# Layer 3's weight product of a four-layer graph network by two levels of Strassen, with weight factors streamed from DRAM

## The chip, the core and the metric

The kernel runs on one of the eight cores of a Trainium2 chip, in float32 throughout. The metric is the device time of that core for one launch, in microseconds (us); lower is better. Five engines work side by side, each through its own queue in order: TensorE (PE, the matrix unit, with its weight loads shown apart as PEld), VectorE (DVE), ScalarE (ACT), GpSimd (POOL), and SyncE (SP), which here only issues DMAs.

## The reference, cut to what matters

Input x holds 128 graphs of 64 nodes with 512 features; adj holds a 64x64 matrix for each graph. Four residual layers follow one another, each as `x = x + layer(relu(layernorm(x)), adj)`. The change concerns layer 3, of which this is the reference:

```python
Xw = X @ Wv + bv
sj = Xw @ aw[:d, 0]
si = Xw @ aw[d:, 0]
e = jax.nn.leaky_relu(sj[:, None, :] + si[:, :, None] + ab[0], negative_slope=0.2)
alpha_matrix = A * jnp.exp(e)
transition = alpha_matrix / (jnp.sum(alpha_matrix, axis=-1, keepdims=True) + 1e-12)
for k in range(Wk.shape[0]):            # 3
    H = H + Xk @ Wk[k] + bk[k]
    Xk = jnp.einsum('bij,bjd->bid', transition, Xk)
return jax.nn.relu(H)
```

So layer 3 multiplies the 512 features of X, of T X and of T T X (T is the transition matrix of a graph) by three 512x512 weights and adds the three. For a token that is one product of a row of 1536 numbers with a 1536x512 matrix.

## The kernel before

Tokens are worked on in 16 groups of 8 graphs: 512 tokens, four tiles of 128 tokens (two graphs each). Phase 1 runs layers 0 and 1 for all groups and writes x to DRAM (`xmid`, shown as xm in the profile). Phase 2 loads it group by group, runs layers 2 and 3, and stores the output. Weights of phase 1 lie in two areas of SBUF, `WA` and `WB`; phase 2 loads its own over them: WA then holds layer 2's, WB layer 3's (`w3_sb`, lines 247 and 248).

All large weight products use one level of Strassen's scheme in Winograd's form (`strassen`, line 589; `seven`, line 568): seven block products instead of eight, and some additions. For layer 3 the two rows of blocks are two token tiles, the block columns are the halves of the 1536 inputs (6 chunks of 128), and the weight's column halves are 256 wide. Each of the seven products is thus 6 matmuls of a 128x128 stationary operand (the transposed activations, tile `a3`) and a 128x256 moving one (the weights), summed in one PSUM bank (line 607). `layer3` calls it twice for each group, for tiles 0 and 1 and for tiles 2 and 3. The left operands are formed on DVE before each call (`comb`, line 599, four additions of 768 elements). Results leave PSUM through ACT (line 575) and DVE (lines 577, 579, 991); POOL adds the bias (line 987); DVE applies the relu and adds x (line 992), which has stayed in SBUF since the group was loaded for layer 2; then SP stores the tile (line 995). The right operands are formed once, at the start of phase 2 (`combine`, line 384), and stay in SBUF.

The order of instructions is not that of the Python loops. Each operation is recorded as a node with an engine, a planned duration (`c_mm` for matmuls, `c_v` for VectorE), its tiles and a priority: the group's number times a period, plus a hand-set shift for each part of the work (table `AT`). `Graph.run` (line 82) then plays the queues through with these durations, gives tiles their slots, and writes every engine's instructions in the planned order, so work of neighbouring groups and layers is interleaved. SP's DMAs are in this plan as well, one queue in order: a DMA whose tile isn't free yet holds back those behind it. Where the planner sees PE without work for over half a microsecond, `fill` (line 1009) writes matmuls on a constant tile. Slots that phase 2 takes over from phase 1 are listed in `TWO`: the second list of each pair may be used when the last user of the first is done.

Two steps take work to another layout. `transposed` (line 551) turns a 128x512 tile by an ACT copy into 16-bit planes, a DMA transpose and an ACT copy back; layers 2 and 3 use it for each token tile. In layer 3 `lm` (line 973) makes T X and T T X, transposed, with 64-row matmuls.

Of the kernel before, what the change touches and what calls it, by code (L numbers as in the profile page):

```python
# [14 lines left out]
P = 128  # L15
# [3 lines left out]
T = 4  # L19
# [148 lines left out]
def tile_adj_preln_d4(  # L168
# [25 lines left out]
        ([("tmp", [P, D], 4), ("mB", [P, T, C + 1], 1)], [("s3", [P, 3, 6, P], 1)]),  # L194
        ([("z", [P, DH], 2)], [("hT", [P, KD, T * P], 1)]),
        ([("rT", [P, KH, P], 3)], [("vu", [P, 2, D + 1], 2), ("tt", [P, T, 2, C], 2)]),
        ([("s2", [P, 3, 4, P], 1), ("s1", [P, 3, 2, P], 2)], [("a3", [P, 3 * KD, P], 2)]),
        ([("y", [P, D], 2)], [("qT", [P, 2, 2 * P], 2)]),
        ([("mT", [P, KD, P], 3)], [("a3", [P, 3 * KD, P], 1)]),
        ([("row", [P, D], 4)], [("sh", [P, 4, 2, 2 * P], 1)]),  # L200
        ([("wa", [P, D], 1)], [("q", [P, D], 1)]),
    ]
# [29 lines left out]
    WB = const.tile([P, 10752], F32, name="wb_mem")  # L232
# [6 lines left out]
    w2_sb = view(WB, 0, KH, D)  # L239
    w2_x = view(WB, 4096, 3 * 4, D // 2).rearrange("p (i c) o -> p i c o", i=3)  # L240
    w_sb = view(WB, 7168, KD, D)
    w_x = view(WB, 9216, 3 * 2, D // 2).rearrange("p (i c) o -> p i c o", i=3)
# [4 lines left out]
    w3_sb = view(WB, 0, 3 * KD, D)  # L247
    w3_x = view(WB, 6144, 3 * 6, D // 2).rearrange("p (i c) o -> p i c o", i=3)


    def c_mm(n, count):
        return 2 * count * max(n * 2 / 2400 + 0.0025, 0.111)
# [21 lines left out]
    def quad(b):  # L274
# [5 lines left out]
    STRETCH, PERIOD1, PERIOD2 = (2.11, 6.43, 4.5, 0.21), 79.8, 140.53  # L280
    AT = {
        "x0": -1458.56, "apart": 58.27, "w1": -1207.06, "b1": -1268.61, "w2": 312.2, "w": -214.25, "c1": 103.95,
        "l0": -1592.46, "c2": -560.69, "l1": 125.29, "c": 849.04, "g0": -1279.86, "g1": -1456.39, "g2": -589.08,
        "g3": -1259.16, "g": -1258.76, "bq": 321.93, "l3": 56.2, "wg": 1603.23, "w3": 387.13, "beg0": -72.8,
        "beg1": 73.58, "end00": 0.51, "end01": 19.09, "end11": -75.14, "new2": 31.64, "new3": 4.77, "end2": -39.58,
        "end3": -21.31, "load1": -108.19, "load2": 27.97, "m": 12.29, "h0": 9.53, "p0": 10.98, "z0": -29.14,
        "q0": 15.48, "y0": -518.61, "h1": -26.33, "p1": -22.59, "z1": -30.25, "q1": 4.48, "y1": -2.94, "s": -20.64,
# [63 lines left out]
    def x_mid(g, t):  # L351
        return xmid[g, t], [("xmid", g, t)]
# [12 lines left out]
    load_w("w2", w2_sb, W2T)  # L365
    b2_b = load_row(b2)
    part("w")
    load_w("w", w_sb, w)


    wa_b = Buf("wa")
# [758 lines left out]
```

## Time and the profile before

| What | Value |
|---|---|
| Median of three runs | 2377.02 us (2373.26 to 2377.84) |
| Span of the profiled execution, first to last instruction | 2373.3 us |
| PE busy | 2349.7 us, 99% of the span |
| DVE busy | 1742.1 us, 73% |
| ACT busy | 1268.7 us, 53% |
| POOL busy | 958.7 us, 40% |
| DMA traffic | 171.02 MB, mean 72 GB/s |
| Chain that ended last | PE 89%; matmuls of line 607 alone 61% |

The span is what the engines show; the time of a run is the device's own. A busy share counts an engine's instructions only, not its waits. Each float32 matmul of the source appears as two MATMUL records and two LDWEIGHTS records. The duration in a record includes the passage through the array, so that records of matmuls overlap; what one costs in a stream is the distance from its start to the next start. The groups of instructions name the tiles by their program names, joined with an underscore where two phases share memory (`tmp_mB_s` holds layer 3's sums in phase 2). The steady part of phase 2 runs from about 1465 us to 2110 us, nine groups.

### The profile page before, as it was taken

The numbers are of one execution on the slowest core, as the hardware profiler recorded it, in microseconds if no ns is written. First come the engines' busy times: TensorE is split into PE (matmuls) and PEld (weight loads), VectorE is DVE, ScalarE is ACT, GpSimd is POOL, SyncE is SP. The second block draws the span as 40 slices with busy tenths as digits, with TensorE's granted clock in tenths as the row PEclk, the third lists the DMA queues.
The fourth block names the chain that finished last, engine by engine and source line by source line (L and its number), as shares of the span: only waits on it lengthen the run. The fifth ranks groups of instructions, "written<-read, shape, count | busy, mean of one in ns | idle before, by whom it ended". The sixth has DMA issues, their size and how long they took to land.

```text
span 2373.3 us, 33860 instructions
## 1 busy us (share of the span) xinstructions
PE 2349.7 (99%) x12008; PEld 1867.5 (79%) x12008; DVE 1742.1 (73%) x3798; ACT 1268.7 (53%) x1746; POOL 958.7 (40%) x1514
## 2 busy tenths in 40 slices
PE   9999999999999999999999999999999999999999
PEld 4677677777677776677788888888888888888887
DVE  7888778788778788777868566666666766667764
ACT  4566656567565576565745445444445444454422
POOL 6244455544455444555443323333323333323330
PEclk9999999999999999999999999999999999999999
DMA  7333222333223333232532322213322223322211
GB/s 258 80 80 65 54 68 64 71 80 63 50 68 69 72 80 54 55 73 71 133 106 59 76 69 61 69 45 69 76 64 65 64 52 73 71 63 65 48 36 40
DMA packets 336922, 171.02 MB, mean 72 GB/s; under 512 B 284656, under 2 KB 290672, under 8 KB 336752
## 3 DMA queue, kind: packets, MB, share of 16 engines
q1 hardware_dynamic: 336752, 168.86, 29.5%
q8 instruction: 94, 1.54, 0.3%
q14 instruction: 76, 0.62, 0.1%
HBM read 66.99 MB, written 34.70 MB: 43 GB/s over the span
## 4 chain that ended last, share of the span: by engine, by line
PE 89%; DVE 5%; DMA 3%; ACT 1%; issue 1%; POOL 1%; SPq 1%; DVEq 0%; ACTq 0%
PE ps L607 61%; PE ps L845 14%; PE ps L546 4%; PE ps L911 2%; PE ps L758 2%; PE ps L973 2%; PE ps L878 1%; DMA x<-xm 1%; DVE st L516 1%; PE ps L957 0%; DMA rw<-row 0%; PE ps L705 0%; DVE tmp_mB_s L599 0%; DVE o L381 0%; PE ps L467 0%
## 5 line engine op out<-in xcount | busy, mean ns | idle before, releaser
L537 ACT ACTIVATE h<-x,nm,rs 128x512 f32<-128x512 f32 x384 | 300.2, 810 | 399.6 <-POOL nm L524 366.8
L607 PE MATMUL ps<-wb_mem,s_s_a 128*128 128x256 f32 x2184 | 512.0, 380 | 0.3
L607 PEld LDWEIGHTS ps<-wb_mem,s_s_a 128*128 128x128 f32 x2184 | 409.5, 190 | 74.0 <-issue 19.8
L518 POOL TENSOR_SCALAR rs<-mv 128x1 f32<-128x1 f32 x320 | 99.2, 310 | 493.0 <-DVE mv L517 477.5
L607 PE MATMUL ps<-wb_mem,tmp_mB_s 128*128 128x256 f32 x1152 | 262.4, 380 | 3.2 <-DVE tmp_mB_s L599 3.1
L607 PEld LDWEIGHTS ps<-wb_mem,tmp_mB_s 128*128 128x128 f32 x1152 | 218.1, 190 | 35.3 <-DVE tmp_mB_s L599 5.4
L607 PE MATMUL ps<-wb_mem,mT_a 128*128 128x256 f32 x1016 | 242.0, 380 | 0.0
L607 PE MATMUL ps<-wa_mem,mT_a 128*128 128x512 f32 x512 | 237.3, 595 | 3.9 <-ACT mT_a L548 3.9
L607 PE MATMUL ps<-wb_mem,rT_vu_tt 128*128 128x256 f32 x1024 | 238.2, 380 | 0.6 <-ACT rT_vu_tt L557 0.6
L607 PEld LDWEIGHTS ps<-wb_mem,rT_vu_tt 128*128 128x128 f32 x1024 | 192.8, 191 | 41.3 <-issue 12.5
L607 PEld LDWEIGHTS ps<-wb_mem,mT_a 128*128 128x128 f32 x1016 | 192.2, 190 | 31.8 <-issue 5.7
L516 DVE BATCH_NORM_STATS2 st<-x 128x6 f32<-128x512 f32 x256 | 173.6, 678 | 45.8 <-DMA x<-xm 40.6
L519 POOL TENSOR_TENSOR rs<-rs,mhalf 128x1 f32<-128x1 f32 x320 | 193.3, 604 | 26.4
L607 PEld LDWEIGHTS ps<-wa_mem,mT_a 128*128 128x128 f32 x512 | 97.1, 190 | 112.7 <-issue 102.4
L607 PE MATMUL ps<-wa_mem,s_s_a 128*128 128x512 f32 x384 | 180.7, 593 | 0.3 <-DVE z_hT L627 0.3
L987 POOL TENSOR_TENSOR u<-u,bk_b 128x256 f32<-128x256 f32 x96 | 76.4, 796 | 238.9 <-DVE u L579 170.2
L575 ACT COPY u<-ps 128x256 f32<-128x256 f32 (+1 forms) x160 | 72.7, 454 | 177.8 <-PE ps L845 105.1
L635 POOL TENSOR_TENSOR u<-u,row_sh 128x256 f32<-128x256 f32 x96 | 74.9, 789 | 228.1 <-DVE u L577 211.6
L733 ACT ACTIVATE z_hT<-z_hT 128x512 f32<-128x512 f32 x128 | 79.6, 627 | 157.8 <-DVE z_hT L627 157.8
L557 ACT COPY rT_vu_tt<-z_hT 128x1024 uint16<-128x1024 uint16 x128 | 147.1, 1159 | 13.7 <-DMA z_hT<-tmp_mB_s 13.3
L546 PEld LDWEIGHTS ps<-bd,h 128*128 128x128 f32 x1024 | 131.1, 192 | 26.6 <-issue 22.2
L524 POOL TENSOR_SCALAR nm<-mv,rs 128x1 f32<-128x1 f32 x320 | 138.5, 433 | 31.1
(174 smaller groups left out, 4336.0 us busy)
## 6 DMA issues: line engine op xcount, KB each, us to landing
x<-in_x_dram SPq DMA_DIRECT2D x64, 256.0 KB, 2.7
xm<-x SPq DMA_DIRECT2D x64, 256.0 KB, 2.1
x<-xm SPq DMA_DIRECT2D x64, 256.0 KB, 2.8
out_dram<-x SPq DMA_DIRECT2D x64, 256.0 KB, 2.0
adj<-in_adj_dram SPq DMA_DIRECT2D x32, 256.0 KB, 4.0
rw<-row SPq DMA_DIRECT2D x94, 64.0 KB, 2.8
wb_mem<-in_Wk_dram SPq DMA_DIRECT2D x6, 512.0 KB, 5.3
tmp_mB_s<-in_Wk_dram SPq DMA_DIRECT2D x8, 256.0 KB, 3.1
```

Of the source, the lines that this page charges most:

```text
L516: dve(0.69, lambda i=i: nc.vector.bn_stats(st.t[:, i, :], src(i)), [r[i]], [(st, i)])
L518: pool(0.32, lambda: nc.gpsimd.tensor_scalar_add(rs.t, mv.t[:, 1:2], EPS), [mv], [rs])
L519: pool(0.65, lambda: nc.gpsimd.tensor_tensor(rs.t, rs.t, mhalf, ALU.pow), [rs], [rs])
L524: pool(0.47, lambda: nc.gpsimd.tensor_scalar(nm.t, mv.t[:, 0:1], rs.t, -1.0, op0=ALU.mult, op1=ALU.mult), [mv, rs], [nm])
L537: act(0.82, lambda: nc.scalar.activation(h.t, xx.t, AF.Relu, bias=nm.t, scale=rs.t), [xx, nm, rs], [h])
L546: nc.tensor.matmul(quad(p)[:, c, :], h.t[:, c * P:(c + 1) * P], rhs(), start=True, stop=True)
L557: act(1.16, lambda: nc.scalar.copy(u16(dst()).rearrange("p c (k q) -> p c k q", q=2), u16(back()).rearrange("p (q c r) -> p c r q", q=2, c ...
L607: nc.tensor.matmul(p.t[:, :n], lhs()[:, c, :], rhs(c), start=first and c == 0, stop=c == kc - 1, skip_group_check=True)
L635: pool(0.75, lambda: nc.gpsimd.tensor_add(U.t[:, iv], U.t[:, iu], row()[:, cols]), [u, krow], [v])
L733: act(0.63, lambda: nc.scalar.activation(z.t[:, cols], z.t[:, cols], AF.Relu), [(z, j)], [(z, j)])
L845: nc.tensor.matmul(pair(p.t)[:, o, :], a, b, start=first and o == 0 and c == 0, stop=c == 1, skip_group_check=True)
L987: pool(0.88, lambda: nc.gpsimd.tensor_add(U.t[:, iv], U.t[:, u[1]], add()), [u, ka], [v])
```

## The change

Layer 3's product becomes two nested levels of Strassen for all four token tiles of a group together, and everything it needs changes with it:

- The outer level's rows are the pairs of tiles (0, 1) and (2, 3), its columns the two 256-wide halves of the 512 features in each of X, T X, T T X. The inner level has the two tiles of a pair and the 128-wide halves of those. There are 7 outer products (`product`), each of 7 inner ones, each of those 3 matmuls of 128x128 by 128x128: 147 for a group.
- A product's seven inner results go to two PSUM banks, four and three blocks of 128 columns. The outer sums are made by further accumulation in these banks: chain X takes products 1, 6, 5 and 3, chain Y products 2, then 7 and 4. ACT copies the intermediate states of X out (`snapshot`), DVE adds the Y states to them (`plus`), POOL does the inner sums and the bias (`emit`, five additions), and DVE does relu and residual.
- Left operands: DVE forms some outer blocks (`minus`, 768 elements, six instructions) and three inner ones for each product (384 elements). Two sums that Strassen needs are made before the transposition, on `h` (half tiles; tile 1, tile 3 and the pair 2, 3).
- Right operands: 49 weight factors of 384x128. In phase 1 `setup_w3` loads the pieces of Wk, forms the factors on POOL in two new slots `wp`, and writes them to DRAM (`fac`). Each product loads two blocks, of 768 KB and 576 KB, into three slots `wf`. WB, the weight loads and the `combine` at the start of phase 2 go.
- x is loaded a second time in phase 2, before layer 2 adds its result to it, so that the slot of the first load is free after the layer norm.
- Slots: phase 1's `rT` goes from 3 to 2; the new layer 3 tiles take over memory from others; WB becomes the tags `w2m` and `wm`, whose successors `a3` and `wf` may start when all of phase 1's uses of them are over.
- The planner's constants are new: the matmul cost, periods, stretches and the table `AT`, and with them the order of everything, in phase 1 too.

```diff
     TWO = [
-        ([("tmp", [P, D], 4), ("mB", [P, T, C + 1], 1)], [("s3", [P, 3, 6, P], 1)]),
+        ([("tmp", [P, D], 4), ("mB", [P, T, C + 1], 1)], [("xi", [P, 3, 3, P], 2)]),
-        ([("rT", [P, KH, P], 3)], [("vu", [P, 2, D + 1], 2), ("tt", [P, T, 2, C], 2)]),
-        ([("s2", [P, 3, 4, P], 1), ("s1", [P, 3, 2, P], 2)], [("a3", [P, 3 * KD, P], 2)]),
+        ([("rT", [P, KH, P], 2), ("wp", [P, 4, P], 2)], [("vu", [P, 2, D + 1], 2), ("tt", [P, T, 2, C], 2)]),
+        ([("s2", [P, 3, 4, P], 1), ("s1", [P, 3, 2, P], 2)], [("zz", [P, 8, P], 3)]),
...
-        ([("mT", [P, KD, P], 3)], [("a3", [P, 3 * KD, P], 1)]),
+        ([("mT", [P, KD, P], 3)], [("sx", [P, 2, 3, 2 * P], 1)]),
...
+        ([("w2m", [P, 7168], 1), ("wm", [P, 3584], 1)], [("a3", [P, 3, KD, P], 4), ("wf", [P, 4, 3, P], 3)]),
...
-        return 2 * count * max(n * 2 / 2400 + 0.0025, 0.111)
+        return 2 * count * max(n * 2 / 2400 + 0.0045, 0.1115)
...
-    STRETCH, PERIOD1, PERIOD2 = (2.11, 6.43, 4.5, 0.21), 79.8, 140.53
+    STRETCH, PERIOD1, PERIOD2 = (2.6483, 3.2376, 6.9527, 0.0065), 98.8, 156.601
...
-        return xmid[g, t], [("xmid", g, t)]
+        return xmid[g, t], [("xmid", g, t)] + ([("xo", g - 1, t)] if g else [])
...
+        bkv = bk3_b.rearrange("p (j n c) -> p j n c", j=2, n=2)
+        dve(0.42, lambda: nc.vector.tensor_sub(bkv[:, :, 1], bkv[:, :, 1], bkv[:, :, 0]), ["bk3"], ["bk3"])
...
+    fac = [[dram.tile([P, n * 3 * P], F32, name=f"fac{f}_{n}") for n in (4, 3)] for f in range(7)]
+    BLOCKS, FACS = ((1, 2, 6, 5), (7, 3, 4)), ((0, 2), (0, 1))
...
+    def setup_w3(f, k):
...
+        sub, turn = nc.gpsimd.tensor_sub, ["wpturn"]
+        src = lambda i, j: Wk3[k].rearrange("(c p) o -> p c o", p=P)[:, 2 * i:2 * i + 2, j * 2 * P:(j + 1) * 2 * P]
+
+        def load(i, j, key=()):
+            b = Buf("wp")
+            dma(256, lambda: nc.sync.dma_start(b.t.rearrange("p (q n) k -> p q (n k)", q=2), src(i, j)), [], [b, *key])
+            return b
+
+        def minus(y, x_, out):
+            pool(1.3, lambda: sub(out.t, y.t, x_.t), [y, x_], [out])
+
+        def factors(F):
+            R = Buf("wp")
+            pool(0.8, lambda: sub(R.t[:, 1:3], F.t[:, 1::2], F.t[:, 0:2]), [F], [R, *turn])
+            pool(0.53, lambda: sub(R.t[:, 0], F.t[:, 3], R.t[:, 1]), [F, R], [R])
+            pool(0.53, lambda: sub(R.t[:, 3], F.t[:, 2], R.t[:, 0]), [F, R], [R])
+            to = lambda n: fac[f][n].rearrange("p (r k c) -> p r k c", k=3, c=P)[:, :, k, :]
+            for n, d, b, v in ((0, slice(0, 2), F, slice(0, 3, 2)), (0, slice(2, 4), R, slice(0, 2)),
+                               (1, slice(1, 2), F, slice(3, 4)), (1, slice(0, 3, 2), R, slice(2, 4))):
+                dma(128, lambda n=n, d=d, b=b, v=v: nc.sync.dma_start(to(n)[:, d], b.t[:, v]), [b], [("fac", f, n, k, d.start)])
+
+        terms = (((0, 0),), ((1, 0),), ((1, 1),), ((0, 0), (0, 1), (1, 1), (1, 0)), ((0, 0), (0, 1)),
+                 ((0, 0), (0, 1), (1, 1)), ((0, 1), (1, 1)))[f]
+        F = load(*terms[0], turn)
+        for at in terms[1:]:
+            Y = load(*at, turn)
+            minus(Y, F, F)
+        factors(F)
...
-            xx, ps, rd, v_ = xt[g, t], [Buf("ps"), Buf("ps")], Buf("ve"), vb[t // 2]
+            xx, ps, rd, v_ = Buf("x"), [Buf("ps"), Buf("ps")], Buf("ve"), vb[t // 2]
+            at, key = x_mid(g, t)
+            part("load3")
+            dma(256, lambda xx=xx, at=at: nc.sync.dma_start(xx.t, at), [*key, (PT, 0)], [xx, ("xo", g, t)])
+            part("pv")
+            xt[g, t] = xx
...
-            for h, b in zip(hh, a3[t0:t0 + 2]):
+            for t, h, b in zip((t0, t0 + 1), hh, a3[t0:t0 + 2]):
+                hv = lambda h=h: h.t.rearrange("p (j q k) -> p j q k", j=2, q=2)
+                if t >= 2:
+                    dve(0.42, lambda hv=hv: nc.vector.tensor_add(hv()[:, 0], hv()[:, 0], hv()[:, 1]), [h], [h])
+                if t % 2:
+                    dve(0.42, lambda hv=hv: nc.vector.tensor_add(hv()[:, :, 0], hv()[:, :, 0], hv()[:, :, 1]), [h], [h])
...
-                        b.t[:, KD:, half].rearrange("p (j c) k -> p c j k", j=2),
+                        b.t[:, 1:, :, half].rearrange("p j c k -> p c j k"),
...
-            def emit_o(i, j, p, u, v, t0=t0):
-                xx, cols, (U, iv) = xt[g, t0 + i], slice(j * D // 2, (j + 1) * D // 2), v
-                add, ka = (lambda: bk3_b[:, cols]), "bk3"
-                if u is not None:
-                    pool(0.88, lambda: nc.gpsimd.tensor_add(U.t[:, iv], U.t[:, u[1]], add()), [u, ka], [v])
-                    add2, ka = (lambda: U.t[:, iv]), v
-                else:
-                    add2 = add
-                dve(c_v(D // 2), lambda: nc.vector.tensor_add(U.t[:, iv], p.t[:, :D // 2], add2()), [p, ka], [v])
-                dve(c_v(D // 2), lambda: nc.vector.scalar_tensor_tensor(xx.t[:, cols], U.t[:, iv], 0.0, xx.t[:, cols], op0=ALU.max, op1=ALU.add), [v, xx], [(xx, j)])
-                if (i, j) in ((1, 0), (0, 1)):
-                    r = (g * T + t0 + i) * P
-                    dma(256, lambda: nc.sync.dma_start(out[r:r + P, :], xx.t), [(xx, 0), (xx, 1)], [])
-
-            ak = {}
-            for i in range(2):
-                b = a3[t0 + i]
-                ak[i, 0] = [(b, 0), (b, 1), (b, 2)]
-                ak[i, 1] = [(b, 1), (b, 2)]
-            part("b0" if t0 == 0 else "b1_")
-            strassen(lambda i, j, t0=t0: a3[t0 + i].t[:, 6 * j:6 * j + 6, :], ak, W3, 6, D // 2, "s3", emit_o)
+
+        part("b0")
+        sx = Buf("sx")
+        keys = lambda i, v: [(a3[2 * i + v], n) for n in range(3)]
+        block = lambda i, j: [(lambda v=v: a3[2 * i + v].t[:, :, 2 * j:2 * j + 2, :]) for v in range(2)]
+
+        A00 = block(0, 0), [[*keys(0, v), (a3[v], "00")] for v in range(2)]
+        A01 = block(0, 1), [[*keys(0, v), (a3[v], "01")] for v in range(2)]
+        S1 = block(1, 0), [keys(1, v) for v in range(2)]
+        A11 = block(1, 1), [keys(1, v) for v in range(2)]
+        S2 = [(lambda v=v: sx.t[:, v].rearrange("p k (q c) -> p k q c", q=2)) for v in range(2)], [[(sx, v)] for v in range(2)]
+
+        def minus(y, x_, blk, kd):
+            for v in range(2):
+                dve(c_v(6 * P), lambda v=v: nc.vector.tensor_sub(blk[v](), y[0][v](), x_[0][v]()), [*y[1][v], *x_[1][v]], [kd[v]])
+
+        banks = {}
+        inner = lambda p, n: p.t[:, :n * P].rearrange("p (r c) -> p r c", r=n)
+
+        def product(f, F, chain, first):
+            (A, B), (ka, kb) = F
+            if first:
+                banks[chain] = [Buf("ps"), Buf("ps")]
+            X = Buf("xi")
+            lo, hi = (lambda f_: f_()[:, :, 0, :]), (lambda f_: f_()[:, :, 1, :])
+            x2, x3, x4 = ((lambda i=i: X.t[:, i]) for i in range(3))
+            sub = nc.vector.tensor_sub
+            dve(c_v(3 * P), lambda: sub(x2(), lo(B), lo(A)), [*ka, *kb], [(X, 0)])
+            dve(c_v(3 * P), lambda: sub(x3(), hi(B), x2()), [*kb, (X, 0)], [(X, 1)])
+            dve(c_v(3 * P), lambda: sub(x4(), hi(A), x2()), [*ka, (X, 0)], [(X, 2)])
+            lhs = {1: (lambda: lo(A), ka), 2: (lambda: hi(A), ka), 6: (x2, [(X, 0)]), 5: (lambda: lo(B), kb),
+                   7: (x3, [(X, 1)]), 3: (x4, [(X, 2)]), 4: (lambda: hi(B), kb)}
+            for n in range(2):
+                w_, p, q = Buf("wf"), banks[chain][n], len(BLOCKS[n])
+                shift = G.shift
+                part("ws")
+                dma(q * 192, lambda n=n, w_=w_, q=q: nc.sync.dma_start(
+                    w_.t[:, :q].rearrange("p r k c -> p (r k c)"), fac[f - 1][n]), [("fac", f - 1, n, k, d) for k in range(3) for d in FACS[n]], [w_])
+                G.shift = shift
+                for r, b in enumerate(BLOCKS[n]):
+                    at, kl = lhs[b]
+
+                    def mm(at=at, r=r, p=p, w_=w_, q=q):
+                        for k in range(3):
+                            nc.tensor.matmul(inner(p, q)[:, r, :], at()[:, k, :], w_.t[:, r, k, :], start=first and r == 0 and k == 0,
+                                             stop=k == 2, skip_group_check=True)
+                    pe(c_mm(P, 3), mm, [*kl, w_] if first and r == 0 else [*kl, w_, p], [p])
+                    step(c_mm(P, 3))
+
+        def snapshot(chain):
+            Z = Buf("zz")
+            for n, p in enumerate(banks[chain]):
+                q = len(BLOCKS[n])
+                act(q * P / 1200 + 0.17, lambda n=n, p=p, q=q: nc.scalar.copy(Z.t[:, 4 * n:4 * n + q], inner(p, q)), [p], [(Z, n)])
+            return Z
+
+        def plus(Z, chain):
+            for n, p in enumerate(banks[chain]):
+                q = len(BLOCKS[n])
+                dve(c_v(q * P, True), lambda n=n, p=p, q=q: nc.vector.tensor_add(Z.t[:, 4 * n:4 * n + q], inner(p, q), Z.t[:, 4 * n:4 * n + q]), [p, (Z, n)], [(Z, n)])
+
+        def emit(i, j, Z):
+
+
+            z = lambda a, b, s=1: Z.t[:, a:b:s]
+            add = nc.gpsimd.tensor_add
+            cast = lambda n: z(n, n + 1).to_broadcast([P, 2, P])
+            pool(0.8, lambda: add(z(0, 4, 3), z(0, 4, 3), bk3_b[:, 2 * j * P:2 * (j + 1) * P].rearrange("p (a b) -> p a b", a=2)), [(Z, 0), "bk3"], [(Z, 0)])
+            pool(0.8, lambda: add(z(1, 3), z(1, 3), cast(0)), [(Z, 0)], [(Z, 0)])
+            pool(0.8, lambda: add(z(0, 8, 7), z(3, 5), cast(2)), [(Z, 0), (Z, 1)], [(Z, 0), (Z, 1)])
+            pool(0.53, lambda: add(z(4, 5), z(7, 8), z(3, 4)), [(Z, 0), (Z, 1)], [(Z, 0), (Z, 1)])
+            pool(0.8, lambda: add(z(2, 4), z(5, 7), z(0, 8, 7)), [(Z, 0), (Z, 1)], [(Z, 0), (Z, 1)])
+            cols = slice(2 * j * P, 2 * (j + 1) * P)
+            for v in range(2):
+                xx = xt[g, 2 * i + v]
+                dve(c_v(D // 2), lambda v=v, xx=xx: nc.vector.scalar_tensor_tensor(
+                    xx.t[:, cols], Z.t[:, 1 + 2 * v:3 + 2 * v].rearrange("p a b -> p (a b)"), 0.0, xx.t[:, cols], op0=ALU.max, op1=ALU.add), [(Z, 0), (Z, 1), xx], [(xx, j)])
+                if (i, j) in ((0, 1), (1, 0)):
+                    r = (g * T + 2 * i + v) * P
+                    dma(256, lambda xx=xx, r=r: nc.sync.dma_start(out[r:r + P, :], xx.t), [(xx, 0), (xx, 1)], [])
+
+        minus(S1, A00, S2[0], [k[0] for k in S2[1]])
+        product(1, A00, "X", True)
+        s0 = snapshot("X")
+        minus(A11, S2, A00[0], [k[-1] for k in A00[1]])
+        product(2, A01, "Y", True)
+        plus(s0, "Y")
+        emit(0, 0, s0)
+        product(6, S2, "X", False)
+        s1 = snapshot("X")
+        minus(A01, S2, A01[0], [k[-1] for k in A01[1]])
+        product(5, S1, "X", False)
+        s2 = snapshot("X")
+        product(3, A01, "X", False)
+        s3 = snapshot("X")
+        emit(0, 1, s3)
+        product(7, A00, "Y", True)
+        plus(s2, "Y")
+        emit(1, 1, s2)
+        product(4, A11, "Y", False)
+        plus(s1, "Y")
+        emit(1, 0, s1)
 
     def step(us):
 
...
+    for i in range(21):
+        G.prio = ((i + 1.0) * (NG - 2.0) / 21) * PERIOD1
+        part("wp")
+        setup_w3(i // 3, i % 3)
...
-    part("w3")
-    for k in range(3):
-        src = Wk3[k].rearrange("(c p) o -> p c o", p=P)
-        for c in (0, 2):
-            i = k * KD + c
-            dma(512, lambda i=i, c=c, src=src: nc.sync.dma_start(w3_sb[:, i:i + 2, :], src[:, c:c + 2, :]), [], [("w3", i // 2), *olds("w2", KH)])
-    W3 = combine("w3", w3_sb, w3_x, 6, D // 2, "DVE", [*olds("w2", KH), *olds("w", KD)])
```

## The prediction, made before the changed kernel was run

> **What bounds the kernel now.** I read the page's busy shares first, then the table by stretches for the steady part of phase 2, then PE's waits, and last the timeline for the distance between matmuls. In the stretch line the columns are window, length, then busy us with the count for PE, PEld, DVE, ACT and POOL, granted clock, DMA share, GB/s. A wait line gives total us, times, longest.
>
> ```profile
> PE 2349.7 (99%) x12008; PEld 1867.5 (79%) x12008; DVE 1742.1 (73%) x3798; ACT 1268.7 (53%) x1746; POOL 958.7 (40%) x1514
> 1464.90:2109.50 644.60, 642.60 (x3889) 561.97 (x3888) 434.21 (x955) 305.13 (x414) 213.29 (x342) 1.00 0.28 65
> PE ps L607 <- ACT mT_a L548: 3.9, 1, 3.9
> PE ps L957 <- DVE rT_vu_tt L948: 3.4, 3, 1.5
> PE ps L607 <- DVE tmp_mB_s L599: 3.1, 4, 1.1
> ```
>
> Over nine groups of the steady part PE idles 2.0 us of 644.6 and its longest waits in the whole run are a few microseconds. So each group costs what its matmuls cost: 644.6 / 9 = 71.6 us. DVE is at 67% there (48.2 us a group), ACT 47% (33.9), POOL 33% (23.7), DMA 28%. Only less PE time shortens a group.
>
> A busy PE says nothing of what a matmul costs; the distance between starts in the timeline does (start, length, instruction):
>
> ```profile
> 311.28 1.05 PE L546 MATMUL ps<-bd,h 128*128 128x128 f32 x8
> 312.17 3.62 PE L607 MATMUL ps<-wb_mem,rT_vu_tt 128*128 128x256 f32 x16
> ...
> 1701.86 2.75 PE L607 MATMUL ps<-wb_mem,tmp_mB_s 128*128 128x256 f32 x12
> 1704.45 5.34 PE L845 MATMUL ps<-row_sh,wa_mem 128*128 128x256 f32 x24
> ...
> 2253.62 0.84 PE ps L957 x8
> ```
>
> Twelve records of width 256 take 2.59 us, 215.8 ns each; eight of width 128 take 0.89 us, 111.3 ns; and L957, only 64 wide, needs 0.84 / 8 = 105 ns. So width 128 is nearly twice as cheap as 256, but a narrower matmul gains nothing more.
>
> **What the Trainium skill says.** The page TensorE: Matmul & The Clock Gate, section LDWEIGHTS (loading the stationary operand), has a weight load take its columns / 1.2 ns, about 107 ns for 128 columns. That fits the floor of 105 to 111 ns above: at width 128 the matmul has come down to its weight load. SBUF — State Buffer, section SBUF: two separate sides, says that a DVE operation with two SBUF inputs and a GpSimd operation lock each other out of a shared port. The trace agrees: of the same 768-element additions some take 946 ns and others 1373.
>
> ```profile
> L599 DVE TENSOR_TENSOR tmp_mB_s<-s_s_a 128x768 f32<-128x768 f32 x12 | 11.4, 946 | 0.0
> L599 DVE TENSOR_TENSOR s_s_a<-s_s_a 128x768 f32<-128x768 f32 x6 | 8.2, 1373 | 0.0
> L991 DVE TENSOR_TENSOR u<-ps,u 128x256 f32<-128x256 f32 x55 | 23.2, 422 | 35.9 <-PE ps L607 25.8 <-POOL u L987 9.8
> L987 POOL TENSOR_TENSOR u<-u,bk_b 128x256 f32<-128x256 f32 x54 | 42.6, 788 | 120.4 <-DVE u L579 81.4 <-DVE x L992 37.6
> x<-xm SPq DMA_DIRECT2D x64, 256.0 KB, 2.8
> 35.00:40.00 5.00, 4.74 (x18) 2.62 (x17) 4.96 (x7) 2.42 (x4) 3.42 (x7) 1.00 1.01 370
> SPq L995 <- DVE x L992: 175.5, 50, 22.9
> ```
>
> (The group lines give busy us and mean ns after the bar; the DMA line ends with us from issue to landing.) DMA: Bandwidth & Descriptors, section Specifications, names 358 GB/s as a core's share of HBM; the start of this run moved 370 GB/s with the DMA engines full, so I use 370. The same page, section Anatomy of one DMA — SWDGE (gpsimd) path, says that a DMA's semaphore wait is done on the issuing sequencer before dispatch. The trace agrees: SP stood 175.5 us in front of output stores, with everything behind them held.
>
> **The change, part by part.**
>
> *Matmuls.* Removed: 84 matmuls of width 256 a group, 1344 in all, two records each: 2688 x 215.8 ns = 580.1 us. Added: 147 of width 128, 2352 in all: 4704 x 111.3 ns = 523.6. Filler matmuls go from 82 to 93 in the two programs' PE queues: 22 more records, 2.4 us. Sum -54.1 us, all on the bounding engine. The arithmetic falls by an eighth but the time only by 10%, since width 128 sits at the weight load's floor. That pitch held over eight records in the trace; I take it for runs of over a hundred.
>
> *DVE, per group.* Out: eight L599 additions (78.1 us / 9 = 8.7), eight L991 (3.4), four L577/L579 (1.7): 13.8. In: six of 768 elements (5.7 at 946 ns), 21 of 384 (between the 422 ns of 256 elements and 946: 553 ns, 11.6), three PSUM additions of 512 (2.0) and three of 384 (1.7), four half-tile ones (1.7): 22.7. Relu and residual stay at eight of 256. So 48.2 + 8.9 = 57.1 us, plus collisions with POOL: at the 427 ns that separates the two L599 rows, on a quarter of some 45 two-input operations, 5 us. That makes 62 us in a group of 68: 91%, hidden, but with little room. Bounds of the collisions: nothing, or every one of them (19 us).
>
> *POOL and ACT.* POOL loses six L987 (4.7 us) and gains four sets of four 256-element additions at 788 ns and a half one (about 0.5): 14.6. That is 33.6 us of 68, and PE waits for these sums only through the three `zz` slots. ACT gains eight PSUM copies of 0.48 to 0.6 us and loses two: 37.5 us. Both are hidden. But products 6, 5 and 3 follow each other on the same banks, so each copy must be out while the other half-product runs (2.0 us or more).
>
> *Weight stream.* 49 x 196,608 bytes = 9.63 MB a group, 26 us at 370 GB/s, beside the 20 us of DMA time there now (0.28 x 71.6) and 2.8 us for the second x loads: 49 of 68 us. Capacity suffices; timing is close. In PE's new queue products 6, 5, 3, 7 and 4 run nearly back to back, with four L845-type groups of 1.73 us among the first. A slot freed by one half-product is needed again two half-products later, 12 x 2 x 111.3 + 9 x 2 x 111.3 ns = 4.67 us. A 256 KB load lands in 2.8 us, of which its bytes take 0.7; so 768 KB needs 2.1 + 2.1 = 4.2 us, 576 KB 3.7, and some 0.2 us for the semaphore. It fits by 0.3 us if nothing is in the way. In SP's queue, though, between loads of products 5 and 3 stand an x load and transposes for the next group that wait for ACT, and a transpose lands in 3.1 us. If ACT or DVE is late, the weights behind it are, and PE waits for them. Bounds: 0 to 8 us a group; I take 1.0, so 16 us in all, with DVE's delays in it. Two other waits are new on SP. The output stores wait for POOL's longer sums; behind them stand the first loads of the next group, needed some 30 us later. The second x loads wait for layer 2's attention tile; behind them stand the next group's first x loads and, a little later, its weights, and DVE's line for layer 2's result waits for the loads themselves. I count both in the same 0 to 8.
>
> *Start of phase 2.* The four W3 additions and six loads go from the crowded turn of phases. Instead `a3` and `wf`, thus every layer 3, must wait for the last use of W2 and W. The PE queue has 60 filler matmuls around that turn against 43, so more gaps were planned there. Bounds 0 to 10; I take +4.
>
> *Phase 1.* Same matmuls. POOL gains 21 sets of (0.79 + 2 x 0.5) us and 21 additions of 1.4: 67 us over 1187, from 49% to 54% busy; SP gains 126 DMAs, some 20 MB. `rT` with two slots binds the next pair's transposes to the end of this pair's product. PE has other groups' work in its queue; I take 0, bounds -3 to +10.
>
> *End.* Now the last matmul is followed by two DVE operations of 0.42 us and the store. Then: a 384-element DVE addition (0.55), three of POOL's five additions (2.1), two of DVE (0.86). +3 us.
>
> Sum: -54.1 + 16 + 4 + 0 + 3 = -31 us. From the profiled 2373.3: 2342. The median of the runs is 3.7 us above that execution, so 2346. A steady group should come to 71.6 - 3.5 + 1.0 = 69.1 us.
>
> **Rivals.**
>
> A (forecast), PE still bounds, a third of its gain is lost: 2346. Chance 0.48.
>
> B, the plan holds and the waits stay as rare as now: -54.1 + 3 = -51: 2326. For it: PE waits hardly at all today in equally tight chains. Against it: nothing today streams on the critical path. 0.20.
>
> C, slower: the weight loads come late. With three slots, a landing d later than the 4.67 us costs d for every three half-products, and ten of them stand in the dense stretch: 3.3 d a group. It outweighs the gain from d = (54.1 - 7) / 16 / 3.3 = 0.9 us, a landing of 5.6 us. At 6.3 us: 85 us, so -54 + 7 + 85 = +38: 2415. For it: SP's order, and only 0.3 us in hand. Against it: DMA half idle over the group, and layer 2 matmuls between. 0.16.
>
> D, DVE becomes the second bound: if half of the 45 operations collide, 57.1 + 9.6 = 66.7 us beside PE's 68; two queues this full can't both run without gaps, and the group goes to about 70: 2377 - 16 x 1.6 + 7 = 2358. For it: both L599 rows. Against it: phase 1 runs PE at 99% beside a DVE at 80%. 0.14.
>
> E, the change leaves PE's work as it was: excluded by its queue (2352 new matmuls for 1344); equal times by chance 0.02.
>
> **How the numbers follow.** A difference under 0.2% (4.7 us) can't be told from none. Faster: A, B and 0.10 of D, 0.78. Within 0.2%: 0.02 of D, 0.01 of C and E, 0.05 in all. Slower: the other 0.15 of C and 0.02 of D, 0.17. The range 2320 to 2386 runs from B, with a little for phase 1, to C's first third; the likeliest case alone spans 2332 to 2362.
>
> **What will show it.** Right: width-128 rows of the new product at 111 to 112 ns from start to start, groups of 69 us, waits for `wf` of a microsecond or so. Wrong: a pitch above 115 ns in long runs (+20 us for each 4 ns), PE waits for the weight DMA of tens of microseconds in total (C), waits for DVE sums with DVE over 90% (D), or idle PE in phase 1.

## The result, and the profile after

The changed kernel takes 2452.1 us (2450.4 to 2460.2), the kernel before 2376.3 in the same series: a ratio of 1.033, interval 1.031 to 1.035. It is slower by 76 us, where 30 us less were forecast. The profiled execution spans 2450.7 us, 77.4 more than before's 2373.3.

The busy shares of the changed kernel's page:

```profile
PE 2335.0 (95%) x14046; PEld 1896.0 (77%) x14046; DVE 1973.5 (81%) x4067; ACT 1320.1 (54%) x1842; POOL 1238.1 (51%) x1822
PE 44%; DVE 19%; POOL 14%; DMA 10%; ACT 6%; issue 5%; SPq 1%; POOLq 0%; DVEq 0%; ACTq 0%
```

PE was 99% busy and is 95% busy. The second line gives the shares of the chain that ended last: PE had 89% of it and has 44%. No one engine took its place; DVE, POOL and DMA share most of the rest.

The table by stretches for eight groups of the steady part (columns as in the prediction):

```profile
1531.90:2128.50 596.60, 558.99 (x4465) 513.91 (x4464) 497.27 (x985) 297.15 (x416) 306.12 (x416) 0.99 0.73 206
```

A group takes 596.6 / 8 = 74.6 us (before 71.6), of which PE idles 4.7. DVE is at 83%, 62.2 us a group; the DMA engines, 28% busy before, are at 73%. The DMA view of the same stretch shows that this mean hides two halves (busy tenths in 40 slices, GB/s, then KB and median us from issue to landing):

```profile
DMA  4889538896388963989538895397972889529896
GB/s 66 244 264 280 151 84 238 257 267 171 95 238 236 294 167 95 242 271 270 153 93 240 272 267 202 66 249 255 270 198 76 230 254 280 181 64 247 251 272 201
...
w2m_wm_a_wf<-fac SPq DMA_DIRECT2D x56, 768.0 KB, 5.3
w2m_wm_a_wf<-fac SPq DMA_DIRECT2D x56, 576.0 KB, 5.0
```

Each group fills the DMA engines to 80 or 90% for some three fifths of its time, at 240 to 290 GB/s, and leaves them half empty for the rest. The weight blocks land in 5.3 and 5.0 us. PE's waits in the whole run, longest totals first (total us, times, longest):

```profile
PE ps L882 <- DVE u L616: 20.1, 11, 2.3
PE ps L1074 <- DMA w2m_wm_a_wf<-fac: 14.2, 13, 2.1
PE ps L795 <- DVE y_qT L674: 11.9, 10, 1.2
PE ps L1074 <- ACT h L574: 7.9, 5, 2.1
PE ps L953 <- DVE rT_wp_vu_tt L938: 6.3, 13, 1.2
PE ps L644 <- DVE u L616: 6.1, 4, 4.4
```

There is no large wait to point at, only many of one or two microseconds, behind DVE, the weight DMA and ACT. Line 882 is a product of layer 2, not touched by the change.

Where the 77.4 us arose, from the starts of unchanged matmuls (the last pair of aggregations of phase 1, `M` times `y`; the transition product T T at the head of layer 3), in us:

| Stretch | before | after | difference |
|---|---|---|---|
| start to phase 1's last aggregation | 1180.1 | 1212.0 | +31.9 |
| from there to the fourth group's T T product | 284.8 | 319.9 | +35.1 |
| eight steady groups | 573.2 | 596.6 | +23.4 |
| the rest | 335.2 | 322.1 | -13.1 |

The second and the fourth row belong together, because the new order also moves matmuls from behind the marks to before them. It shows in the run e6 below, where PE hardly waits: PE is busy for 296.5 us of its second stretch, against 279.0 before, and for 292.7 us of its last, against 328.5.

### The profile page after: what moved, and what is told of

It is laid out like the page before. It is cut to its first block, busy times and chain, and to the rows that moved or that the text cites. A ratio compares the mean times of both kernels' runs of the same rounds, so it can differ in the third digit from the quotient of the medians.

```text
span 2450.7 us, 39373 instructions
## 1 busy us (share of the span) xinstructions
PE 2335.0 (95%) x14046; PEld 1896.0 (77%) x14046; DVE 1973.5 (81%) x4067; ACT 1320.1 (54%) x1842; POOL 1238.1 (51%) x1822
## 4 chain that ended last, share of the span: by engine, by line
PE 44%; DVE 19%; POOL 14%; DMA 10%; ACT 6%; issue 5%; SPq 1%; POOLq 0%; DVEq 0%; ACTq 0%
PE ps L644 20%; PE ps L1074 9%; PE ps L882 7%; POOL rs L556 3%; PE ps L583 3%; DMA w2m_wm_a_wf<-fac 2%; POOL nm L561 2%; ACT h L574 2%; DVE s_s_zz L636 2%; PE ps L1020 2%; PE ps L795 2%; POOL x L759 2%; DVE st L553 2%; PE ps L953 2%; DMA x<-xm 2%
## 5 line engine op out<-in xcount | busy, mean ns | idle before, releaser
L1074 PE MATMUL ps<-w2m_wm_a_wf 128*128 128x128 f32 x2304 | 300.6, 277 | 10.2 <-DMA w2m_wm_a_wf<-fac 4.9
L1074 PEld LDWEIGHTS ps<-w2m_wm_a_wf 128*128 128x128 f32 x2304 | 279.1, 192 | 15.3 <-DMA w2m_wm_a_wf<-fac 4.2
L1074 PE MATMUL ps<-w2m_wm_a_wf,tmp_mB_xi 128*128 128x128 f32 x2016 | 267.0, 278 | 22.5 <-DMA w2m_wm_a_wf<-fac 9.1
L644 PE MATMUL ps<-w2m_wm_a_wf,s_s_zz 128*128 128x256 f32 x1152 | 274.4, 380 | 2.9 <-DVE s_s_zz L636 2.0
L1074 PEld LDWEIGHTS ps<-w2m_wm_a_wf,tmp_mB_xi 128*128 128x128 f32 x2016 | 246.9, 193 | 31.2 <-ACT h L574 15.4
L644 PEld LDWEIGHTS ps<-w2m_wm_a_wf,s_s_zz 128*128 128x128 f32 x1152 | 217.2, 190 | 42.8 <-DVE s_s_zz L636 7.0
L644 PE MATMUL ps<-wa_mem,mT_sx 128*128 128x512 f32 x512 | 236.9, 597 | 7.2 <-DVE u L616 5.8
L644 PE MATMUL ps<-w2m_wm_a_wf,rT_wp_vu_tt 128*128 128x256 f32 x1024 | 240.3, 380 | 3.5 <-ACT u L612 2.1
L644 PEld LDWEIGHTS ps<-w2m_wm_a_wf,rT_wp_vu_tt 128*128 128x128 f32 x1024 | 191.0, 190 | 43.4 <-issue 11.2
L644 PE MATMUL ps<-wa_mem,s_s_zz 128*128 128x512 f32 x384 | 178.8, 594 | 3.7 <-DVE s_s_zz L636 2.3
```

The lines of the kernel that those rows point to most:

```text
L644: nc.tensor.matmul(p.t[:, :n], lhs()[:, c, :], rhs(c), start=first and c == 0, stop=c == kc - 1, skip_group_check=True)
L1074: nc.tensor.matmul(inner(p, q)[:, r, :], at()[:, k, :], w_.t[:, r, k, :], start=first and r == 0 and k == 0, stop=k == 2, skip_group_check ...
```

## The experiments

Four theories were held against each other. S: the weight stream comes late. L: DVE and POOL hold each other up (the shared port). O: the fixed order is at fault; when one wait goes another comes. B, formed after the first four runs: stream and DVE with POOL are both full, so that each holds the group when the other is removed. In the first twelve runs every engine keeps the changed kernel's order; only what an entry writes is taken away or swapped.

### One load removed at a time

```diff
+ e1: a wf slot is loaded only the first time it is used
+ e2: POOL's five additions in emit write nothing
+ e3: DVE's inner subtractions x2, x3, x4 are made once per slot
+ e4: POOL's subtractions in setup_w3 write nothing
```

> The changed kernel in the same planned order, but each of the three wf slots is loaded once and all later weight loads are left out, so layer 3's product uses wrong weights. Theory S (the weight stream comes late and holds SP's queue): PE waits for the weights end, and so do late transposes and x loads behind them; 2452 falls by 60 us or more, to 2390 or less. Theory L (DVE is late because GpSimd's longer sums and DVE's two-input operations lock each other out): only the direct waits for the weight DMA go, about 18 us of extra distance between matmuls in the changed kernel's trace; 2425 to 2440. Theory O (the new order itself leaves too little slack, whatever the load): also 2425 to 2440.

> The changed kernel in the same planned order, with POOL's five additions of each emit left out (20 a group, 320 in all): the inner sums and the bias are missing from the output. Theory L: collisions between DVE and POOL in phase 2 go back to about what they were before (56 us there against 144 in the changed kernel), DVE comes in time; 2452 falls by 45 to 80 us. Theory S: POOL's sums stand only before stores; less than 15 us. Theory O: less than 15 us.

> The changed kernel in the same planned order, with DVE's three 384-element subtractions per product made only once for each xi slot (15 or so of 336 remain), so layer 3's left factors are wrong. DVE loses 11.6 us and 21 two-input operations a group. Theory L: DVE is no longer late; 2452 falls by 50 to 90 us. Theory S: less than 20 us. Theory O: less than 20 us.

> The changed kernel in the same planned order, with POOL's subtractions in setup_w3 left out (84 operations of phase 1; the DMAs stay, the stored factors are wrong). The question is phase 1, which took 43 us longer to the first layer 3 work of phase 2 (1308 against 1264.5 us). Theory L: collisions with these POOL operations made it late; 15 to 35 us of the 43 come back. Theory O: the new order of phase 1 with two rT slots made it late; under 10 us come back, since POOL's factors are finished in the first third while the waits go on to the end of phase 1.

Measured: 2441.9, 2438.0, 2436.9 and 2444.9 us; ratios to the kernel before 1.028, 1.026, 1.026, 1.029, each within 0.004. Each removal gives 7 to 15 us (e4's 7 is not clear of the noise: its interval overlaps the changed kernel's), and the steady group stays at 74.4, 74.8, 73.4 and 74.6 us. So S alone and L alone both fall; what O had forecast for the four holds to within 2 us. In e4 the first T T product comes at 1298.6 us in place of 1308.0: 9 of the 43 us come back, on O's side of the line. Without the stream (e1, first two lines) PE waits for DVE; without the additions (e2, third line) it waits for the stream, and the DMA view of e2's steady groups is as full as ever:

```profile
PE ps L882 <- DVE u L616: 26.3, 12, 2.3
PE ps L1076 <- DVE s_s_zz L1091: 17.3, 14, 1.4
PE ps L1074 <- DMA w2m_wm_a_wf<-fac: 19.4, 22, 2.6
DMA  9799367893689837898378983778935889367983
```

### Two loads together

> Leaves out two things at once, in the changed kernel's own order: the weight factors are loaded once per slot instead of 98 times a phase-2 pass, and GpSimd's five emission additions per outer block are gone. Alone the first gave 10 us and the second 14. Theory B (two bounds beside each other: the stream fills the DMA engines, and VectorE with GpSimd is full as well, so that each holds the group when the other is taken away): much more than the sum, about 2390 us (2375 to 2405), the group near 70 us. Theory O (the fixed order and its latency chains hold the group, whatever is taken out): about the sum of the two, 2428 us (2420 to 2438), the group still near 73 us.

> As the run before it, and VectorE's three inner subtractions per product (21 a group) are made only once per buffer as well: three parts of the work are left out. Theory B: about 2375 us (2360 to 2390), the group near 68.5 us, which is TensorE's own work. Theory O: about the sum of the three single gains (10 + 14 + 15), 2413 us (2405 to 2425).

> Leaves out the five emission additions and the 21 inner subtractions, and keeps the stream of weight factors. Theory B: the stream alone still holds the group, so little more than either alone, about 2432 us (2425 to 2440), with waits for the weight loads grown past 25 us in all. Theory O: about the sum of the two, 2423 us or less. Theory L (VectorE's and GpSimd's collisions hold it): about 2400 us or less.

(The 98 loads named here and below are a slip: there are 14 loads a group, 224 in all.) Measured: 2364.7 (ratio 0.997, 0.996 to 0.999), 2361.2 (0.996, 0.994 to 0.998) and 2436.0 (1.027, 1.023 to 1.031). Removing both gives 87 us where the single gains add up to 24 (84 us by the ratios: the kernel before ran 5 us faster in this series). That is B, and more than B had forecast; O's forecast for e6, about the sum, falls. The steady stretch of e6:

```profile
1511.60:2059.60 548.00, 545.50 (x4465) 509.75 (x4465) 450.46 (x985) 297.44 (x416) 171.81 (x256) 1.00 0.35 84
```

PE is busy 545.5 of 548.0 us, and a group takes 68.5 us, 3.15 less than before's 71.65. This is the gain that the matmuls were forecast to give (54.1 / 16 = 3.4). With the subtractions gone too the group is still 68.5: PE's own work. With the stream left in (e8) it is 74.5.

A part of these differences is PE's clock. In the changed kernel a wait of 2.16 us ends at 1593.18 us; for the next 3.4 us the granted clock is 0.50, and eight records of width 256 take 3.66 us where the next eight take 1.89:

```profile
1593.18 3.66 PE L882 MATMUL ps<-row_sh,wa_mem 128*128 128x256 f32 x8 [2.16 <-DVE u L616]
1596.67 1.89 PE L882 MATMUL ps<-wa_mem,row_sh 128*128 128x256 f32 x8
1593.20:1596.60 3.40, 3.40 (x8) 2.77 (x9) 0.69 (x1) 0.00 (x0) 2.03 (x2) 0.50 0.85 243
```

So a wait can cost about 1.7 us more than its length. After the first 100 us and up to the last matmul, 5 such stretches of 3.4 us are in the changed kernel's trace, 9 in e1's and 8 in e2's (one of 6.8 us in each counted twice), none in e6's and 2 in that of the kernel before. At 1.7 us each, an estimate from these lines, e1 and e2 would have gained some 17 and 19 us with the changed kernel's five, and e6 would still have gained 79. The clock makes the single gains look smaller than they are; it doesn't make up the difference.

### What in the stream, and what in the additions

```diff
- w_.t[:, :q]...          <- fac[f - 1][n]                      (e9, on e2)
+ first half of its bytes <- first half of fac[f - 1][n]
- nc.gpsimd.tensor_add(...) five times in emit                  (e10, on e1)
+ nc.gpsimd.memset(Z..., 0.0) of 720 or 480 columns
```

> Leaves out the five emission additions, and of each of the 98 loads of weight factors per phase-2 group pair only the first half of the bytes is moved (384 and 288 KB in place of 768 and 576); the number of loads, their places in SP's queue and their waits stay. With the additions gone and whole loads the time was 2438, with no loads at all 2365. If it is the bytes (the DMA engines are full in the product's stretch): 2370 us (2362 to 2380) and landings of about 3 us. If it is the loads' waits for their slots and SP's in-order queue, whatever their size: 2420 us or more.

> The weight factors are loaded once per slot, and each of GpSimd's five emission additions per outer block is replaced by a GpSimd memset of about its length (720 columns for 770 ns, 480 for 530 ns), which keeps its place, its waits and those who wait for it, and reads nothing. With the additions in place the time was 2442, without them 2365. If the harm is that VectorE and GpSimd hold each other up when both read SBUF: 2370 us (2360 to 2385). If it is that the additions stand in GpSimd's queue and in the chain snapshot, additions, residual, store: 2435 us or more.

Measured: 2371.4 us (0.999, 0.998 to 0.999) with half the bytes, against 2438.0 with all of them and 2364.7 with none; landings 3.6 and 3.3 us in the steady part. The steady group takes 69.4 us. The number of loads and the order in SP's queue were the same, so it is the bytes. And 2379.1 us (1.002, 1.000 to 1.003) with memsets, against 2441.9 with the additions: POOL's queue had as many operations of about the same length (698 ns for a memset of 720 columns), the chain was the same, and 63 of the 77 us between e1 and e6 were gone; the steady group takes 69.5 us. The group rows of the residual operation (busy us, mean ns of one) in the steady stretch, first e1 with POOL's additions, then e10 with memsets:

```profile
L1107 DVE SCALAR_TENSOR_TENSOR x<-s_s_zz,x 128x256 f32<-128x256 f32 x64 | 43.8, 713 | 13.8 <-POOL s_s_zz L1103 13.8
```

```profile
L1107 DVE SCALAR_TENSOR_TENSOR x<-s_s_zz,x 128x256 f32<-128x256 f32 x64 | 31.3, 519 | 9.9 <-POOL s_s_zz L1103 9.9
```

The same instruction takes 713 or 519 ns, by what POOL does beside it; in e6, where POOL does neither, it takes 519 as well. The changed kernel's timeline shows one case (start, length):

```profile
1879.73 0.94 DVE L1105 SCALAR_TENSOR_TENSOR x<-s_s_zz,x 128x256 f32<-128x256 f32 x1
...
1879.57 0.82 POOL L1097 TENSOR_TENSOR s_s_zz<-s_s_zz,bk_b 128x256 f32<-128x256 f32 x1
```

POOL began first and ends at 1880.39, 0.66 us after DVE's start. DVE's operation, 0.42 us when alone, lasts 0.94: it waited 0.52 us, about the remaining 0.66 less 0.13.

### Phase 1

```diff
+ e11, on e6: setup_w3 writes its loads, subtractions and stores only for f = 0
```

> On top of the kernel without stream and without emission additions (2365 us, first product of the layer-3 neighbour matrix at 1304 us): setup_w3 is done only for the first of the seven outer factors, so 18 of its 21 pieces are left out with their loads, GpSimd subtractions and stores. If the 43 us that phase 1 lost against the kernel before (1265 to 1308) are the setup's own work in GpSimd's and the DMA queue, that mark comes at about 1270 and the time is about 2330 us. If it is the other order in which the plan puts phase 1's unchanged work, the mark stays at 1293 to 1300 and the time is 2353 to 2362 us.

Measured: 2349.4 us (0.989, 0.986 to 0.992), the mark (the first T T product) at 1291.5 us, 12.4 earlier than in e6; both lie between the two forecasts. Phase 1's last pair of aggregations starts at 1195.5 (e6 1208.7, before 1180.1). A group of phase 1 still takes 73.4 us, before 71.9. The setup's work costs some 13 us by these marks (15 by the medians), all of it in about the first third of the phase. The remaining 15 us of phase 1 are neither its PE work (busy 1168 us, before 1171) nor the setup; the order was left as a suspect.

### The additions on DVE

```diff
-            add = nc.gpsimd.tensor_add
+            add = nc.vector.tensor_add        (e12; e13 on e1)
```

> The whole work; the five emission additions per outer block run on VectorE in place of GpSimd, at the same places of the order (20 additions a group, about 8.1 us of VectorE's time). If collisions with GpSimd are what the additions cost, they go, the stream still holds the group, and the time falls to about 2438 us. If VectorE has no room for them, 2465 to 2485 us.

> As the run before it, with the weight factors loaded once per slot. If VectorE has room for the additions: 2385 to 2400 us, group 70 us. If not: about 2470 us, as with the stream, and TensorE waits for VectorE.

Measured: 2440.0 us (1.027, 1.024 to 1.030), the whole work, 12 us faster than the changed kernel; and 2409.3 (1.014, 1.011 to 1.017) without the stream, 33 less than e1. So the lock costs more than the additions' own 8 us on DVE. The 2409 lies between the two forecasts, the steady group at 71.5 us: the room is there in part, and PE waits for DVE's sums again (15.8 us for `u`, 10.1 for `zz`).

### The same work in another order

Whether B's two bounds are bounds at all, or only made so by the order, is told by changing the order alone.

```diff
-        for _, _, o in order:
-            if o.seq in idle:
-                fill(*idle[o.seq])
-            o.fn()
+        for i in ORDER:                   # a table of the 10,623 operations
+            self.ops[i].fn()
```

The tables come from a search that moved operations within their queues in a replay of the five queues. The replay's durations and delays were taken from the traces above; its times are no evidence, the runs are. The instructions and slots stay, except that the planner's filler matmuls are left out. From the second table on, the replay charged the lock as read above and 275 GB/s for loads.

> The whole work with the same instructions in the same buffers (the plan's filler matmuls excepted), but each engine and SP's queue take them in another fixed order, one that was sought by moving instructions about until TensorE's waits fell when a GpSimd addition and a VectorE operation on SBUF that overlap are charged half of the overlap, and a transfer is charged at 315 GB/s. If the two resources are bounds whatever the order (the DMA engines full, VectorE and GpSimd full): no better than 2430 us, the group at 73 us or more. If the fixed order leaves TensorE waiting because it puts the stream and the additions where they collide, though both have room over the whole group: 2350 to 2400 us, the group at 69 to 71 us.

> The whole work of the changed kernel, same instructions and buffers (fillers excepted), in a second searched order on each engine. The search now charges what the traces of the earlier runs show: a GpSimd or VectorE operation on SBUF alone that starts second waits for the first to end (less 0.13 us), and 275 GB/s for loads. If order is most of the loss, this is faster than the first searched order (2410): 2360 to 2395 us. If 2410 is already near what the two resources allow: 2400 us or more.

> A control: the kernel before, same instructions and buffers (fillers excepted), in an order searched in the same way. If the search only undoes what the change put wrong, the kernel before gains nothing or little (2365 to 2376 us), for TensorE was 99% busy. If it gains as well, down to 2335 to 2360 us, part of what the searched orders give the changed kernel is not owed to the change.

> The whole work of the changed kernel (fillers excepted), in an order put together from two: phase 1's own work in the order of the kernel before, setup_w3 placed in it, and phase 2 as in the second searched order; then searched again, mostly around the start and the turn of the phases. If phase 1's loss (25 us by the fifth group, 1.6 us a group after that) is order but for the setup's 14 us, the mark of the ninth aggregation pair comes at 370 to 380 us (before 361, after 387), its groups take 72 us, and the time is 2365 to 2385 us. If it isn't the order, 2395 to 2405 as in the second searched order.

> As the run before it, from another start of the search; the same numbers are expected, and the difference between the two shows how much of such a result is chance.

| Kernel | us | ratio to before | phase 1's last pair of aggregations | steady group |
|---|---|---|---|---|
| before | 2376 | 1 | 1180.1 | 71.65 |
| changed | 2452.1 | 1.033 (1.031 to 1.035) | 1212.0 | 74.6 |
| changed, first order (o1) | 2410.1 | 1.015 (1.013 to 1.017) | 1203.7 | 71.2 |
| changed, second order (o2) | 2397.7 | 1.009 (1.008 to 1.011) | 1215.1 | 70.6 |
| before, searched order (o3) | 2377.9 | 1.001 (1.000 to 1.002) | 1184.1 | 71.7 |
| changed, joined order (o4) | 2374.1 | 0.999 (0.999 to 1.000) | 1196.6 | 71.1 |
| changed, joined order, other start (o5) | 2381.6 | 1.003 (1.002 to 1.004) | 1199.3 | 70.9 |

Another order, without the filler matmuls, takes the changed kernel from 2452 to 2374 us, level with the kernel before, whose own time a searched order without fillers doesn't lower. So the two bounds bind in this order and far less in another: nearly all of the 76 us can be had back with every byte, addition and subtraction still there. o1 and o2 missed their forecasts (2350 to 2400, 2360 to 2395) by 10 and 3 us; o4's (2365 to 2385) held. The fillers are 186 records, some 21 us of PE's time, and none of them stands in the eight steady groups: the 28 us gained there (596.6 to 568.8) are order. How much of the other 50 us is owed to the missing fillers was not measured in the changed kernel. In o4 a group of phase 1 takes 72.1 us with PE busy 718.7 of 721 us, so that part of phase 1's loss was order too. The steady stretch and the loads' landings of o4:

```profile
1500.70:2069.50 568.80, 551.39 (x4465) 510.77 (x4464) 472.82 (x984) 297.95 (x416) 302.33 (x416) 1.00 0.78 216
```

```profile
DMA  7986749986698686898758988589855978759886
...
w2m_wm_a_wf<-fac SPq DMA_DIRECT2D x56, 768.0 KB, 5.5
w2m_wm_a_wf<-fac SPq DMA_DIRECT2D x56, 576.0 KB, 4.6
```

The loads take as long as in the changed kernel. But the DMA row's low digits, which were 2 to 5 in every group, are now mostly 5 and 6: the same bytes are spread over more of the group. DVE's busy time falls from 62.2 to 59.1 us a group; 2.3 of these 3.1 us come from fewer meetings with POOL's additions (85 two-operand operations held up in place of 119). PE idles 2.2 us a group in place of 4.7.

That o4 and o5, equal by their expectations, differ by 7 us shows how much in such a table is chance. No version that does the whole work was found to beat the kernel before by more than a measurement can tell.

## Why the prediction was wrong, point by point

- *Matmuls, -54.1 us: right.* The median distance between the new product's records is 112 ns, in the changed kernel as in e6, and e6's groups are 3.15 us shorter than before's. In the chain of the changed kernel's group at 1905 us a run of 54 records costs 113 ns each:

```profile
1938.15 6.12 PE ps L1074 x54
```

- *DVE, 62 us a group: the sum was right, the word "hidden" was not.* It measured 62.2. Delays by the lock, costed at 5 us a group, are about 7 in phase 2 (113 us in 241 operations that started behind a POOL operation; before 30 us in 56). But an engine at 83% in this fixed order isn't hidden: its results come late one by one, as PE's waits in e1 show.
- *POOL, 33.6 us: 38.3.* The price of 788 ns already held some delay. POOL's operations that start behind DVE's lost 124 us in phase 2, 7.8 a group.
- *Weight stream, +1.0 us a group: this is the step that failed.* The DMA's share, 49 of 68 us (72%), came true at 73%. The landings didn't: 4.2 and 3.7 us were put in, at 370 GB/s, and 5.3 and 5.0 were measured, at 240 to 290 GB/s with DMA engines shared with transposes and x loads. They exceed the 4.67 us that a slot allows. The term held DVE's delays too, and for both together the steady group loses 74.6 - 68.5 = 6.1 us in place of 1.0. The bound of 8 us held it; the value taken did not. Over 16 groups, if all lose as the eight steady ones do, these 5.1 us are 82 of the 107 us between forecast and result. The late landing is not the whole mechanism: o4's loads land no sooner and its group loses 2.6 us.
- *Start of phase 2, +4 (0 to 10): not shown to be wrong.* From phase 1's end to the fourth group the time grew by 35 us. Of these 17 belong to the stream and the additions (e6: 302.9 for 319.9), and as many are PE's own work, which the new order has put ahead of the mark and taken from the last stretch. PE idles 6.4 us there in e6 and 5.8 before, so that the turn of the phases itself costs next to nothing beyond its matmuls.
- *Phase 1, 0 (-3 to +10): the second step that failed.* It lost 32 us. Some 13 are the setup's work; most of the rest is the order (o4 has it at +16.5 with the setup in it, and `rT` still with two slots; 66 filler records are gone there too). A new table `AT` was read as harmless because the matmuls were the same.
- *End, +3: right.* From the last matmul's end to the last instruction it takes 7.3 us in place of 4.0.

Of the rivals, C had the late loads and D the second bound, and each was priced alone and too low. With the stream and no additions (e2) the group takes 74.8 us at landings of 5.7 and 5.1 us, where C's formula for 5.7 adds some 3.4 us to PE's 68.5; with the additions and no stream (e1) it takes 74.4, where D said about 70. So 87 us stood behind two conditions of which either was enough. C's counter-argument, "DMA half idle over the group", didn't fit the forecast's own 49 of 68 us. DVE and POOL were priced by their mean over a group, with no question of when within the group they are used. The loads' timing was asked about, but at the 370 GB/s of the run's start. And the planner's order, whose durations hold neither lock nor contention, was taken as if it would adapt.

## What to carry to other kernels

In a kernel whose engines follow orders fixed beforehand, a resource with some room on average can still hold the bounding engine, as the DMA engines at 73% and DVE at 83% did here: look at its share in the stretch where it is used, not over the period. When removing one suspect gains little, remove two at once before acquitting either; gains that don't add up show resources that bind side by side. And if a planner writes the order, the durations it believes, contention among them, are part of the kernel: try the same work in another order before taking the work away.

## What the runs showed of the hardware

- The lock between DVE and POOL goes by who is first. In the changed kernel 335 DVE operations with two operands in SBUF began while a two-operand POOL operation more than one column wide had over 0.2 us to go. They took 0.47 us longer on average, and 91% of them by that remainder less 0.13 us, to within 0.05. 293 operations that read PSUM took no longer in the same position, nor did 68 of the layer norm's statistics (`BATCH_NORM_STATS2`), nor 101 two-operand operations beside a POOL operation of one column. The one that began first lost nothing (0.007 us over 94 DVE operations). It holds the other way too: 425 two-operand POOL operations behind DVE's, those of one column among them, lost 0.30 us each.
- A POOL memset does far less harm than an addition of about the same length: 2379 against 2442 us. In e10's trace 117 two-operand DVE operations that began beside such a memset took no longer than alone.
- The DMA engines were 90% and more busy at 240 to 290 GB/s in the mixed load of phase 2, where loads at the start of the kernel before had reached 370.
- After some waits of PE its granted clock was halved for 3.4 us, and the distance between records of width 256 was then 427 ns in place of 216. In the changed kernel, after the first 100 us, this followed 5 of 20 waits of 1.5 us or more; which ones is open.
